# Sums of rows packed into four column groups, and the mean of h moved one column tile earlier, in a graph-attention plus mixture-of-experts kernel

## The chip, the cores and the metric

The kernel runs on one core of one Trainium2 chip. The metric is the device time of one execution in microseconds (us); the median of three runs before the change is 1255.57 us. Engines are named as in the profile: PE is TensorE (PEld its weight loads), DVE is VectorE, ACT is ScalarE, POOL is GpSimd, SP is SyncE.

## What is computed

Cut to what matters here (N = 4096 nodes, 256 features, 4 heads of 64):

```
xn   = layernorm(x)
h    = einsum('nd,hdk->hnk', xn, W)
e    = leaky_relu(s_row[:, :, None] + s_col[:, None, :]);  e = where(adj > 0, e, -9e15)
att  = softmax(e);   out = att @ h  (heads side by side)
y    = elu(out) + xn @ Wr + br;   x = x + layernorm(y)
x    = x + moe_ffn(layernorm(x))         # 8 experts, the best 2 for each token
```

A row of `adj` without any edge gives equal attention to all nodes, so its result is the mean of h. The kernel provides for that with a tiny constant: it adds `hbar = TINY * sum-of-xn/N @ W` to every numerator and `TINY` to every denominator. The mean of h needs the sum over all 4096 rows of xn. That small side computation is all that the change touches.

## The kernel before

**Stages.** An opening prepares the first two blocks of 512 nodes by hand. Then come four row blocks of attention (`for a in range(NR)`, each for 1024 target rows in two halves of 512), each running over 32 column tiles `j` of 128 source nodes. After that the experts' layers run, one tile of 256 rows after another.

**One column tile** (lines 1195 to 1238 and 1697 to 1706): DVE makes four weight tiles `w` (L1701, one per head, 128x1024 for both halves; 128x512 where only one half is done), in ten rotating buffers. PE multiplies them: `acc` (L1202, two 32-column pieces of h per head and half) and `den` (L1211, two columns of `unit` per head and half). The pieces are placed in the four 32-column groups of the array so that four run side by side. In the first and the last tile of a row block `attend` takes `other_heads` before `first_heads`, so that `acc` of heads 2 and 3 and `den` are done first. ACT turns the adjacency into a mask `am` for each tile (L1618, three buffers).

**The opening** (`first_phase`, L924 to 1024): block 0 and block 1 are centred, turned and projected without being scaled by 1/deviation first; the factor r is put in later. So their sums of rows can't come for free from the copies that turn the blocks; `sums_of_centred` (L874) takes them with products. For each of 8 pieces (two blocks of 4 x 128 rows) it multiplies the piece by its column of r, one row of 256 results in PSUM, all 8 accumulated in it. DVE copies that row out (L884). After the first half tile the row is turned by two transposes into `pc` (L891), which DVE copies into `sums[:, :, 0]` (L892). Both functions put their PE instructions into the strict PE order (`order_of`, `queue`).

**The other blocks** 2 to 7: `norm_steps` (L1035) measures a block, `normal_row` (L777) scales its four pieces on ACT with `off` and `r` from DVE (`off` is L769), and PE turns them (`pt`, L784); the copies out of PSUM (L800) sum the rows into `sums[:, :, b]`. `project_steps` (L1092) makes `ph` (L1105) and `pr` (L1057). These steps are placed between column tiles of row block 0 by `prepare_at`. The last block's step is over at column tile j = 27 of row block 0.

**The mean of h** (`mean_of_h`, L1171): DVE adds up `sums` into `xm` (L1174, L1175), PE makes four products of 128x128 weights with one column (`pm`, L1179), DVE scales them into `hbar` (L1183). It is called once, after the last column tile of row block 0. Then `finish_blocks` starts: ACT moves `den` out (`ud`, L1410) and the four `acc` banks (`u`, L1413, adding `hbar`), and PE's next row block accumulates into the same banks, so it waits for those copies.

**Who sets the order.** PE's order is written by hand: every PE instruction of the attention goes through `queue`. In the opening every engine keeps the order of the program (`in_trace_order`). After it, DVE, ACT, POOL and SP get their order from the framework's scheduler when the kernel is built; each engine then runs its list in order and waits at an instruction whose inputs or buffers are not ready. PSUM tiles named by `bank` rotate through three banks.

Of the kernel before, what the change touches and what calls it, by code (L numbers as in the profile page):

```python
# [14 lines left out]
OP = mybir.AluOpType  # L15
# [3 lines left out]
P = 128  # L19
# [25 lines left out]
def gat_then_moe(  # L45
# [19 lines left out]
    nc = tc.nc  # L65
    N, D = x.shape
    H, _, K = W.shape
    E, _, F = W1.shape
    NT = N // P
# [19 lines left out]
    TB = B // P  # L89
    HK = H * K  # L90
    Q = 32
# [11 lines left out]
    ident = const.tile([P, P], F32)  # L103
# [4 lines left out]
    parts = nc.dram_tensor("parts", [NB, H, B], F32, kind="Internal").ap()  # L108
# [110 lines left out]
    def forward(apart, stack):  # L219
# [13 lines left out]
        def large(name):  # L233
            return home[0].tile([P, TB, D], F32, tag="large", name=name, bufs=3)
# [10 lines left out]
        def bank(shape, name):  # L245
            return ps.tile(shape, F32, tag="bank", name=name, bufs=3)
# [286 lines left out]
        def queue(ins):  # L533

            if last[0] is not None:
                tc.add_manual_dep(
                    ins.ins, last[0],
                    mybir.DependencyInfo(
                        mybir.DependencyClass.NoSync, mybir.DependencyReason.DATA
                    ),  # L540
                    reason="the order of the tiles in TensorE",
                )
            last[0] = ins.ins.name
# [3 lines left out]
        def order_of(ins):  # L547

            if ordered[0] or strict[0]:
                queue(ins)  # L550
            return ins.ins
# [67 lines left out]
        with ExitStack() as layer:  # L619
# [42 lines left out]
            all1f = gat.tile([P, P], F32)  # L662
# [46 lines left out]
            def bounds_checked():  # L709

                nc.vector.tensor_reduce(strayed, limit, AX.X, OP.max)
                nc.vector.tensor_scalar(strayed, strayed, 0.5 * SPREAD, None, op0=OP.is_gt)
# [16 lines left out]
            sums = gat.tile([P, DC, NB], F32)  # L729
# [143 lines left out]

            def sums_of_centred(blocks):  # L874

                po = bank([1, D], "po")
                parts = [(xb, r, t) for xb, r in blocks for t in range(TB)]
                for n, (xb, r, t) in enumerate(parts):
                    order_of(nc.tensor.matmul(
                        po, r[:, t : t + 1], xb[:, t, :],  # L880
                        start=(n == 0), stop=(n + 1 == len(parts)),
                    ))
                row = large("row")[:1, 0, :]
                nc.vector.tensor_copy(row, po)  # L884
                return row

            def sums_turned(row):

                pc = bank([P, DC], "pc")
                for c in range(DC):  # L890
                    order_of(nc.tensor.transpose(pc[:, c : c + 1], row[:, ts(c, P)], ident[:1, :1]))  # L891
                nc.vector.tensor_copy(sums[:, :, 0], pc)  # L892
                nc.vector.memset(sums[:, :, 1], 0.0)

            def product_of(b, t, ph):
# [183 lines left out]
            def numbers_made():  # L1079

                if not apart:
                    nc.vector.tensor_scalar(brm, brm, -1.0, None, op0=OP.add)
                made_of_numbers()
# [87 lines left out]
            def mean_of_h():  # L1171

                xm = small.tile([P, DC], F32, tag="xm", name="xm", bufs=1)
                nc.vector.tensor_reduce(xm, sums, AX.X, OP.add)  # L1174
                nc.vector.tensor_scalar(xm, xm, 1.0 / N, None, op0=OP.mult)  # L1175
                pm = bank([P, H // 2], "pm")
                for i in range(H // 2):
                    for c in range(DC):
                        order_of(nc.tensor.matmul(  # L1179
                            pm[:, i : i + 1], wall[:, c, ts(i, P)], xm[:, c : c + 1],  # L1180
                            start=(c == 0), stop=(c == DC - 1),
                        ))
                nc.vector.tensor_scalar(hbar, pm, TINY, None, op0=OP.mult)  # L1183
# [438 lines left out]
            if not apart:  # L1622

                with tc.tile_pool(name="gen", bufs=2) as work:
# [12 lines left out]
                    for b in range(NB):  # L1637
# [4 lines left out]
                        for j in range(NT):  # L1642
# [6 lines left out]
                            for h in range(H):  # L1649
                                nc.vector.scalar_tensor_tensor(  # L1650
                                    top[:, h, :], off, eb[:, j, h : h + 1], top[:, h, :],
                                    op0=OP.add, op1=OP.max,
# [5 lines left out]
                            mx, mx, SLOPE, mx, op0=OP.mult, op1=OP.max  # L1658
                        )
                        for j in range(NT):  # L1660
# [7 lines left out]
                            for h in range(H):  # L1668
                                nc.vector.tensor_scalar(
                                    w[:, h, :], rows[:, h, :], eb[:, j, h : h + 1], None,  # L1670
                                    op0=OP.add,
                                )
                            nc.vector.scalar_tensor_tensor(
                                w, w, SLOPE, w, op0=OP.mult, op1=OP.max
# [16 lines left out]
            else:  # L1691

                with tc.tile_pool(name="sep", bufs=2) as work:

                    def weigh(er, am, j, halves):
                        these = slice(halves[0], halves[-1] + 1)
                        mask = am.rearrange("p (s r) -> p s r", s=HB)
                        w = [[None] * H for half in range(HB)]
                        for h in ORDER:
                            wh = work.tile([P, HB, B], F32, tag="w", name="w", bufs=10)  # L1700
                            marks["w"] = nc.vector.scalar_tensor_tensor(  # L1701
                                wh[:, these], er[:, these, h], eb[:, j, h : h + 1], mask[:, these],
                                op0=OP.max, op1=OP.min,
                            ).ins
                            for half in range(HB):
                                w[half][h] = wh[:, half]
                        return w

                    both = list(range(HB))
                    ers = [er0, er1]  # L1710
                    er = er0
                    pending = None
                    norms, steps_of = {}, {}
                    ordered[0] = strict[0] = True
                    opened = len(nc.cur_bb.bb.instructions)
                    row = first_phase(weigh, norms)
                    in_trace_order(opened)
                    ordered[0] = False
                    with tc.issue_after(marks["w"]):
                        numbers_made()  # L1720
                        bounds_checked()

                    def prepare_at(s):

                        for b in range(2, NB):
                            first = TB * b
                            if first - 3 <= s < first:
                                if b not in norms:
                                    norms[b] = norm_steps(b)
                                next(norms[b], None)  # L1730
                            if first <= s < first + 4:
                                if s == first:
                                    steps_of[b] = project_steps(b, True)
                                next(steps_of[b], None)

                    for j in range(TB):
                        prepare_at(TB + j)
                        attend(weigh(er, first_masks[:, j], j, [1]), j, [1])
                        if j == 0:
                            sums_turned(row)  # L1740
                    for a in range(NR):
                        later = None
                        for j in range(0 if a else TB, NT):
                            attend(
                                weigh(er, load_mask(a, j), j, both), j, both,
                                False if (a, j) == (NR - 1, NT - 1) else None,
                            )
                            if a == 0:
                                prepare_at(TB + j)
                            if pending:  # L1750
                                next(pending, None)
                            if a == 1 and j == 1:
                                turn_biases()
                            if a + 1 == NR and j == 3:
                                with tc.issue_after(marks["w"]):
                                    plan_early()
                                first_tile()
                            if a + 1 == NR and j == 25:
                                turn_first()
                            if a + 1 == NR and j == NT - 1:  # L1760
                                gelu_next(xT0[:, DC - 1, :1])
                            if j == 20 and a + 1 < NR:
                                later = ers[(a + 1) % 2]
                                load_rows(later, (a + 1) * HB, HB, nc.scalar)
                        if a == 0:
                            mean_of_h()
                        er = later
                        if a + 1 < NR:
                            pending = finish_blocks(a)
                            next(pending)  # L1770
                    strict[0] = False
# [359 lines left out]
```

## Time and profile before

| | |
|---|---|
| median of three runs | 1255.57 us (1255.51 to 1255.64) |
| the profiled execution | 1254.18 us, of which the profile's span is 1252.5 us |
| PE busy in the span | 1237.9 us (99%) |
| DVE busy | 845.1 us (67%) |
| ACT busy | 448.2 us (36%) |
| POOL busy | 241.8 us (19%) |
| chain that ended last | PE 94%, DVE 3% of the span |
| sums of rows in the opening (L879) | 16 PE instructions, 43.0 to 46.7 us |
| mean of h (L1179) | 8 PE instructions, first at 255.1, last at 255.9 us |
| row block 0 to 1 | about 255 to 258 us |

How to read it: times are microseconds from the start of the span. A product in fp32 shows as two PE records (the eight products at L879 are 16 records). A line of the timeline gives start, length, engine, source line, operation, output<-inputs, shapes and count, and in brackets the idle time of the engine before it with what ended it. The end of a PE record is modelled, so the distance between the starts of successive records tells the pace better than their length. In the chain and wait views, "issue" is time for which the profile shows no cause.

### The profile page before, as it was taken

What the parts mean: (1) busy time and instruction counts of PE and PEld (TensorE: products, weight loads), DVE (VectorE), ACT (ScalarE), POOL (GpSimd) and SP (SyncE); (2) the same over time, 40 slices, a digit from 0 to 9 for tenths busy, and PEclk for the clock granted to TensorE, in tenths of its full rate; (3) what the DMA queues carried; (4) which work ended last, traced back from release to release, by engine and by line L of the source; (5) the groups of instructions that cost most, each with busy time, mean ns of one, the idle gap of its engine ahead of it and who ended that gap; (6) DMA issues with size and microseconds to landing.
All of it is one profiled execution on the core that took longest, in us unless ns stands there. A gap on an engine that the chain in (4) does not pass through costs nothing.

```text
span 1252.5 us, 22714 instructions
## 1 busy us (share of the span) xinstructions
PE 1237.9 (99%) x8872; PEld 647.5 (52%) x8872; DVE 845.1 (67%) x1566; ACT 448.2 (36%) x918; POOL 241.8 (19%) x217
## 2 busy tenths in 40 slices
PE   9999999999999999999999999999999999999997
PEld 5444444332233332332324423888888876666686
DVE  7998887879999989999999996855111211111110
ACT  4332322165522375322645321533323332222322
POOL 4000000001002601006110015124432222222222
PEclk9999999999999999999999999999999999999999
DMA  6333433436533746334366422868999895455662
GB/s 216 118 119 111 164 114 102 150 121 133 187 105 102 236 114 206 103 102 153 113 159 200 128 81 91 273 169 217 229 251 252 222 230 119 106 137 112 135 163 32
DMA packets 155540, 190.22 MB, mean 152 GB/s; under 512 B 72312, under 2 KB 125680, under 8 KB 155040
## 3 DMA queue, kind: packets, MB, share of 16 engines
q1 hardware_dynamic: 133392, 145.39, 40.1%
q0 software_dynamic: 20544, 36.74, 13.3%
q10 hardware_dynamic: 1488, 6.55, 1.5%
q8 instruction: 71, 1.16, 0.4%
q14 instruction: 45, 0.37, 0.1%
HBM read 155.77 MB, written 29.74 MB: 148 GB/s over the span
## 4 chain that ended last, share of the span: by engine, by line
PE 94%; DVE 3%; issue 1%; ACT 1%; DMA 0%; POOLq 0%; SPq 0%; DVEq 0%; ACTq 0%
PE acc L1202 33%; PE po L1919 18%; PE ph L1885 17%; PE den L1211 17%; PE pr L1057 2%; DVE w L1701 2%; PE ph L1105 2%; PE ptx L1257 0%; DMA early<-lists 0%; PE acc L898 0%; PE pt L784 0%; PE ptr L1503 0%; PE po L1958 0%; PE pl L1268 0%; PE acc L748 0%
## 5 line engine op out<-in xcount | busy, mean ns | idle before, releaser
L1202 PE MATMUL acc<-w,ha 128*32 128x512 f32 x4096 | 669.9, 593 | 1.3 <-ACT u L1413 0.9
L1701 DVE SCALAR_TENSOR_TENSOR w<-er,eb,am 128x1024 f32<-128x1024 f32 x496 | 606.0, 1275 | 31.1 <-PE den L1211 30.9
L1211 PE MATMUL den<-w,unit 128*2 128x512 f32 x2048 | 467.0, 592 | 0.1
L1202 PEld LDWEIGHTS acc<-w,ha 128*32 128x32 f32 x4096 | 184.9, 110 | 292.4 <-issue 253.7
L1618 ACT ACTIVATE am<-adj 128x1024 bf16<-128x1024 int32 x124 | 130.7, 1054 | 346.2 <-DVE w L1701 211.7
L1885 PE MATMUL ph<-xT,w 128*128 128x256 f32 (+5 forms) x864 | 229.9, 423 | 0.2 <-ACT hT L1889 0.2
L1919 PE MATMUL po<-w,hT 128*128 128x256 f32 (+1 forms) x1040 | 229.7, 379 | 0.0
L1889 ACT ACTIVATE hT<-ph,bias 128x256 f32<-128x256 f32 (+5 forms) x216 | 111.1, 517 | 288.1 <-issue 186.2
L1919 PEld LDWEIGHTS po<-w,hT 128*128 128x128 f32 (+1 forms) x1040 | 195.7, 189 | 31.2 <-issue 3.1
L1885 PEld LDWEIGHTS ph<-xT,w 128*128 128x128 f32 x864 | 163.5, 190 | 59.7 <-issue 38.0
L1932 DVE SCALAR_TENSOR_TENSOR o<-po,share,b2s 128x256 f32<-128x256 f32 (+2 forms) x66 | 31.5, 478 | 210.9 <-PE po L1919 182.8
L1211 PEld LDWEIGHTS den<-w,unit 128*2 128x2 f32 x2048 | 93.7, 85 | 148.1 <-issue 139.7
L1944 POOL DMA_INDIRECT out<-o,ids x66 | 102.6, 1554 | 323.3 <-DMA out<-o,ids 141.5
L1388 POOL DMA_INDIRECT lists<-xe,at x64 | 89.3, 1395 | 267.6 <-issue 184.2
L1869 DVE STREAM_TRANSPOSE xT<-xr 128x512 f32<-128x512 f32 (+5 forms) x21 | 17.9, 851 | 70.9 <-PE ph L1885 31.2
L1057 PE MATMUL pr<-wr,xT 128*128 128x256 f32 x128 | 30.4, 381 | 0.2 <-ACT er L1151 0.2
L1907 ACT ACTIVATE b2s<-b2b,share 128x256 f32<-128x256 f32 x68 | 30.0, 499 | 0.0
L1125 POOL DMA_DIRECT2D residual<-rb x6 | 4.7, 784 | 121.2 <-DVE rb L1072 121.2
L1453 POOL DMA_DIRECT2D xf<-in_x x6 | 8.1, 1345 | 102.2 <-ACT xf L1452 102.2
L1057 PEld LDWEIGHTS pr<-wr,xT 128*128 128x128 f32 x128 | 24.1, 190 | 5.4 <-issue 0.9
L1105 PE MATMUL ph<-wall,xT 128*128 128x264 f32 x96 | 24.6, 399 | 0.0
L207 ACT ACTIVATE m<-y,off 128x256 f32<-128x256 f32 x48 | 23.7, 494 | 1.1 <-DVE off L215 0.6
(394 smaller groups left out, 616.4 us busy)
## 6 DMA issues: line engine op xcount, KB each, us to landing
adj<-in_adj SPq DMA_DIRECT2D x126, 512.0 KB
w<-in_L_ffn_W SPq DMA_DIRECT2D x54, 1024.0 KB
er<-parts ACTq DMA_DIRECT2D x3, 2048.0 KB
lists<-zeros POOLq DMA_DIRECT2D x8, 520.0 KB
residual<-rb POOLq DMA_DIRECT2D x8, 512.0 KB
rb<-residual SPq DMA_DIRECT2D x8, 512.0 KB
out<-y POOLq DMA_DIRECT2D x8, 512.0 KB
xb<-in_x SPq DMA_DIRECT2D x7, 512.0 KB
```

The costliest lines, as they stand in the source:

```text
L1057: order_of(nc.tensor.matmul(pr[:, k, :], turned[b][:, c, ts(t0 + k, P)], wr[:, c, :], start=(c == 0), stop=(c == DC - 1),))
L1105: order_of(nc.tensor.matmul(phs[t - t0], xT[:, c, ts(t, P)], wall[:, c, :], start=(c == 0), stop=(c == DC - 1),))
L1202: queue(nc.tensor.matmul(acc[half][h // 2][here : here + Q, :], ha[:, j, h * K + g * Q : h * K + (g + 1) * Q], w[half][h], start=(j == 0), ...
L1211: queue(nc.tensor.matmul(den[here : here + HB, :], unit[:, j, h, 1 - half : 1 - half + HB], w[half][h], start=(j == 0 and half == 0), stop ...
L1388: ins = nc.gpsimd.indirect_dma_start(lists, bass.IndirectOffsetOnAxis(ap=at[:, k, t : t + 1], axis=0), xe[:, t, :], None,).ins
L1618: nc.scalar.activation(am, at, AF.Relu, scale=2.0)
L1701: marks["w"] = nc.vector.scalar_tensor_tensor(wh[:, these], er[:, these, h], eb[:, j, h : h + 1], mask[:, these], op0=OP.max, op1=OP.min,).ins
L1885: order_of(nc.tensor.matmul(ph, job["w1"][:, c, ts(f, P)], xT[:, c, :], start=(c == 0), stop=(c == DC - 1),))
L1889: job["gelu"] = nc.scalar.activation(hT[:, f, :], ph, AF.Gelu, bias=job["bias"][:, f : f + 1]).ins
L1919: order_of(nc.tensor.matmul(po[:size], hT[:, f, k * CH : k * CH + size], w2[:, f, :], start=(f == 0), stop=(f == FC - 1),))
L1932: given_out.append(nc.vector.scalar_tensor_tensor(o[:size], po[:size], share[:size, k : k + 1], b2s[k][:size], op0=OP.mult, op1=OP.add,).ins)
L1944: added.append(add().ins)
```

## The change

The sums of the first two blocks are taken by the same eight products, but each with its column of r repeated 32 times, and the four pieces of a block go to four different groups of 32 PSUM partitions. So PSUM holds 128 rows: 32 equal copies of four partial sums. The DVE copy takes 128 rows. Turning the row is now a product with a column of ones over all 128 partitions, which adds the four partial sums 32 times over; the DVE instruction that stores the result scales it by 1/32. Separately, `mean_of_h` is called after column tile 30 of row block 0 in place of after tile 31.

```diff
-                po = bank([1, D], "po")
-                parts = [(xb, r, t) for xb, r in blocks for t in range(TB)]
-                for n, (xb, r, t) in enumerate(parts):
-                    order_of(nc.tensor.matmul(
-                        po, r[:, t : t + 1], xb[:, t, :],
-                        start=(n == 0), stop=(n + 1 == len(parts)),
-                    ))
-                row = large("row")[:1, 0, :]
+                po = bank([P, D], "po")
+                for n, (xb, r) in enumerate(blocks):
+                    for t in range(TB):
+                        order_of(nc.tensor.matmul(
+                            po[ts(t, Q)], r[:, t : t + 1].to_broadcast([P, Q]), xb[:, t, :],
+                            start=(n == 0), stop=(n + 1 == len(blocks)),
+                        ))
+                row = large("row")[:, 0, :]
                 nc.vector.tensor_copy(row, po)
...
-                    order_of(nc.tensor.transpose(pc[:, c : c + 1], row[:, ts(c, P)], ident[:1, :1]))
-                nc.vector.tensor_copy(sums[:, :, 0], pc)
+                    order_of(nc.tensor.matmul(
+                        pc[:, c : c + 1], row[:, ts(c, P)], all1f[:, :1], start=True, stop=True
+                    ))
+                nc.vector.tensor_scalar(sums[:, :, 0], pc, 1.0 / Q, None, op0=OP.mult)
...
                             if a == 0:
                                 prepare_at(TB + j)
+                            if (a, j) == (0, NT - 2):
+                                mean_of_h()
...
-                        if a == 0:
-                            mean_of_h()
```

## The prediction

> **What bounds the kernel now.** I read the page first: its busy times and the chain that ended last.
>
> ```profile
> PE 1237.9 (99%) x8872; PEld 647.5 (52%) x8872; DVE 845.1 (67%) x1566; ACT 448.2 (36%) x918; POOL 241.8 (19%) x217
> PE 94%; DVE 3%; issue 1%; ACT 1%; DMA 0%; POOLq 0%; SPq 0%; DVEq 0%; ACTq 0%
> ```
>
> PE is the chain nearly everywhere, and its order is fixed by hand. So what PE is spared anywhere before 773 us moves all that follows, as long as nothing else becomes late. Next, the timeline of the opening's end:
>
> ```profile
> 43.03 2.97 PE L879 MATMUL po<-xb,rrow 128*1 128x256 f32 x13
> 43.93 2.73 DVE L1701 SCALAR_TENSOR_TENSOR w<-er,eb,er 128x512 f32<-128x512 f32 x4
> 45.84 0.59 PE L879 MATMUL po<-xb,rrow 128*1 128x256 f32 x2
> 46.27 0.38 PE L879 MATMUL po<-xb,rrow 128*1 128x256 f32 x1
> 46.69 0.41 DVE L884 COPY row<-po 1x256 f32<-1x256 f32 x1
> 47.03 2.72 DVE L1701 SCALAR_TENSOR_TENSOR w<-er,eb,er 128x512 f32<-128x512 f32 x4
> 49.15 0.28 PE L891 MATMUL pc<-ident,row 1*128 1x1 f32 x2
> 49.36 1.06 PE L1202 MATMUL acc<-w,ha 128*32 128x512 f32 x8
> ```
>
> The reader is to see 16 records of `po` one after the other, 0.216 us apart (43.03 to 46.27 in 15 steps), all in the first column group, and DVE without a pause beside them. The waits of DVE from 43 to 99 us hold only one of 0.3 us, before 43.14; PE has none put down to another engine in 43 to 256 us. From 100 us DVE waits for PE again and again (17 times, 14.8 us, at `w`, behind `den`): from there PE alone sets the pace. Last, the border of row blocks 0 and 1, and ACT at the next border, 1 to 2:
>
> ```profile
> 255.12 1.05 PE L1179 MATMUL pm<-xm,wall 128*128 128x1 f32 x8
> 256.10 1.03 PE L1211 MATMUL den<-w,unit 128*2 128x512 f32 x4
> 257.12 0.15 DVE L1183 TENSOR_SCALAR hbar<-pm 128x2 f32<-128x2 f32 x1
> 257.31 2.42 ACT L1413 ACTIVATE u<-acc,hbar 128x512 f32<-128x512 f32 x4 [0.16 <-DVE hbar L1183]
> 258.05 0.62 PE L1202 MATMUL acc<-w,ha 128*32 128x512 f32 x2 [0.92 <-ACT u L1413]
> ```
>
> ```profile
> 428.70 0.69 ACT L1413 ACTIVATE u<-acc,hbar 128x512 f32<-128x512 f32 x1 [0.36 <-PE acc L1202]
> 429.56 0.69 ACT L1413 ACTIVATE u<-acc,hbar 128x512 f32<-128x512 f32 x1 [0.17 <-PE den L1211]
> 430.14 0.68 ACT L1410 ACTIVATE ud<-den,tiny 128x512 f32<-128x512 f32 x1
> ```
>
> At the first border `hbar` sits on DVE behind three `w` and ends at 257.27; the copies `u`, and PE's first `acc`, follow it. At the second, where `hbar` is long there, the copies run while PE is still at the last tile.
>
> [...] the router's 32-column products `pl` (L1268) of 128 columns issue 32 records from 366.34 until `acc` follows at 367.22, 0.11 us for each four. [...] Here the trace shows two `pc` transposes as 2 records, and four `pm` products as 8: an fp32 product costs twice the records.
>
> **The opening, part by part.**
>
> *Products.* 16 records x 0.216 = 3.46 us become 4 rounds of four records. If they run side by side as `pl` and `acc` do (acc rounds are 0.429 us apart at 512 columns), that is 4 x 0.216 = 0.86 us: 2.6 us less. Weight loads of 32 columns take 110 ns against 84, but lie beside products, as in `acc`. If the groups did not overlap the gain would be 0; I take 2.6.
>
> *What is late next: w.* In the built order of the changed kernel the row copy stands before the last of the four `w` of the next half tile (the first three were made by 42 us); before, it stood four `w` later. The copy now waits for `po`: last record 43.68, end 44.06, copy at 44.12 in place of DVE being free at 43.93, a pause of 0.19. It takes a slot of 0.34 (46.69 to 47.03; one partition or 128 should be alike: `ha`, 128x256, takes 0.42 against 0.41 here). So that `w` runs from 44.46 to 45.20. PE, free of `po` at 43.90, does `den` and `acc` of heads 1, 0, 2 until 44.76, then waits for head 3 until 45.25: 0.5 us of the gain lost (the cost today is nothing, because the longer `po` covers it).
>
> *Turning.* Two transposes cost 0.21 (49.15 to 49.36); four records of full products at the pace of `pm` (0.98 for eight) cost 0.49: 0.28 more. `sums` is read far later, at 208 us; a scaling of 128x2 takes 0.152 (hbar) against 0.143 for the copy.
>
> Sum: -2.6 + 0.5 + 0.28 = -1.8 us on PE at about 49 us.
>
> *Does it last until DVE has slack?* PE runs 1.8 earlier, DVE about 0.1 later. The tightest `w` I find in the DVE timeline against the tiles' starts is head 0 of tile 4: ready 55.52, used 58.27, a slack of 2.75. It holds. The second risk is a reordering. In the changed build the statistic `off` of block 3 (81.40 now) stands behind one more `w`, and ACT does the next mask before the four rows of `xb`, not after:
>
> ```profile
> 81.59 2.08 ACT L777 ACTIVATE xb<-xb,off,r 128x256 f32<-128x256 f32 x4 [4.40 <-DVE off L769]
> 83.58 1.04 ACT L1618 ACTIVATE am<-adj 128x1024 bf16<-128x1024 int32 x1
> ```
>
> Today the rows are ready at 83.67 and PE turns them from 86.78: slack 3.1. Changed: that `w` runs to 82.6 (81.48 + 1.27 + about 0.25 of pauses at `sc` and `ha`, less 0.41 for two small instructions that stand later now), the mask 82.65 to 83.7, the rows 83.6 to 85.8; PE wants the last of them at 85.7 (86.78 - 1.8 + 6 x 0.109). So 0.2 us of waiting, within 0 to 0.7 if the DVE pauses are 0.7. After 95 us slack is large again: block 4's rows end by 101 us and are turned at 116 us. I take -1.6 for the opening, ends -1.0 and -1.8. The two earlier `x` loads on SP follow `po` by dependence and are not needed before 62 us.
>
> **The border, part by part.** The eight `pm` records, with the array running empty before them, cost PE 1.1 us (255.01, when the next round was due, to 256.10). Between tiles 30 and 31 they cost the same, since that border is an unbroken stream too: 0. `xm` is done at 208 us, so nothing waits there. What goes is PE's wait: `den` begins at 256.10, `acc` at 258.05, and from 258.05 the tile takes its full 12 rounds (its end at 263.21 is 5.16 later, 12 x 0.429 = 5.15), so the early `den` bought nothing: 1.95 us are lost today. In the changed order `hbar` stands behind the first `w` of tile 1 of the next row block; that is the one at 250.75 today, so `hbar` is made at about 252.1, and `u` can start when heads 2 and 3 are summed, about 253.7. The order of `u`, `u`, `ud`, `u`, mask, `u` is then that of the border 1 to 2, where PE loses nothing: first `den` at 431.06, one round after the last `acc` at 430.63. Gain 1.95; were a copy late by a mask's 1.06 us it would be 0.9, and more than 1.95 can't be had because nothing else waits.
>
> **Sum.** -1.6 - 1.95 = -3.55 us. Against the profiled execution (span 1252.5, total 1254.18): 1250.6; it lies 1.39 us under the median of the runs, so 1255.57 - 3.5 = 1252.1 is what I predict. About 0.2% (2.5 us, down to 1253.06) is what a measurement of this kernel can tell from no change.
>
> **Rivals.**
> 1. *DVE eats the opening's gain.* For: DVE has no pause from 43 to 99 us. Against: its lead is 2.75 us or more. If the pauses add up and PE waits at block 3's turn for 1.2 us more, the opening gives 0.4: 1253.2.
> 2. *The border stays closed for another reason*, say a mask ahead of `u` on ACT. For: a mask of 1.06 stood in front of it (256.09). Against: the border 1 to 2. Only the opening counts: 1254.0.
> 3. *The full opening gain, no wait at block 3 or for head 3*: -2.3 - 1.95: 1251.3.
> 4. *Slower.* The one mechanism: block 3's rows on ACT, behind `off`, one more `w` and a mask, are so late that PE, whose order is strict, stands before `pt`. It costs 1 us for each us beyond 85.7, and outweighs both gains (3.75) when the last row ends after 89.5, that is, when `off` slips by 5 us and not 1.2; two more `w` and a round trip to ACT would do it. At 5 us of waiting: 1256.8.
> 5. *The change doesn't do what it says*: groups not side by side, and the turning dearer: opening +0.3, border -1.95: 1253.9.
>
> **Chances.** Forecast 0.62 (own range 1251.6 to 1252.7); rival 1 0.16, of which half is beyond 1253.06; rival 2 0.08; rival 3 0.06; rival 4 0.05; rival 5 0.03. Faster by over 0.2%: 0.62 + 0.06 + 0.08 = 0.76; within: 0.08 + 0.08 + 0.03 = 0.19; slower 0.05. The range takes in forecast, rivals 3 and 1: 1251.2 to 1253.7.
>
> **What would show it.** `po` records in fours, 0.216 apart, over by 44.1; a PE pause before head 3's `acc` near 44.8; `pc` near 47.1 with four records; the turn of block 3 near 85, with or without a pause; `hbar` near 249 to 252, `u` before the last `acc` of row block 0, and no pause of PE at that border. I am wrong if PE stands before `pt` for over 1 us, if `po` runs in a row, or if the copies `u` still begin after the last tile.

## The result and the profile after

The changed kernel takes 1251.76 us (median of six runs, 1250.76 to 1252.48) against 1255.61 us of the kernel before (median of six): a ratio of 0.9973, 95% interval 0.9962 to 0.9983. Run again in a later set it took 1251.07 us (1250.89 to 1251.43) against 1255.29, ratio 0.997 (0.9958 to 0.9982). The profiled execution of the changed kernel took 1252.34 us with a span of 1250.3. In what follows line numbers of the changed kernel are those of before plus 2 from `sums_turned` on: `acc` is L1204, `w` L1703, `pm` L1181, `hbar` L1185, `u` L1415. Three stages will come up again and again: the *opening* (up to the end of the turning of the sums, about 50 us), the *turn of block 3* (PE turning that block's rows, `pt`, about 87 us) and the *border* between row blocks 0 and 1 (about 255 us). The first product behind the border that belongs to the finished row block is `pd`. Products in the four 32-column groups (`acc`, `den`, now `po`) are called packed, the others (`pt`, `pc`, `pm`, and `pp`, which turns a block's factors) full-array.

The page of the changed kernel, its busy times and the shares of the chain that ended last:

```profile
PE 1235.8 (99%) x8874; PEld 647.2 (52%) x8874; DVE 845.5 (68%) x1566; ACT 448.6 (36%) x918; POOL 242.1 (19%) x217
PE 94%; DVE 3%; issue 1%; DMA 1%; ACT 1%; POOLq 0%; SPq 0%; DVEq 0%; ACTq 0%
```

Hardly anything here tells of the change: PE has two more records (the turning has four in place of two) and is busy 2.1 us less. The page sums over the whole run, so the gain has to be read stage by stage. I take the same PE step in both traces and subtract: how much earlier or later does it start?

| PE's step, at its time before | after minus before, us | what lies behind it |
|---|---|---|
| 8.5 (`pt`, block 0) | -0.26 | start of this execution |
| 20.1 to 43.0 (`po` begins) | +1.36 | halved clock from 8.5 to 12.0, see below |
| 52.1 to 86.8 | -0.31 | opening: -1.67 |
| 93.0 to 234 | -0.24 | turn of block 3: +0.07 |
| 263.3 (`pd`) to 784 | -2.17 | border of row blocks 0 and 1: -1.93 |

A minus sign means earlier. The three stages that the change touches sum to -3.53 us. The step of +1.62 to the second row isn't the change's: PE reaches the first changed product only at 43 us, and the view by windows shows TensorE's clock there. Its columns are the window, its length, then the busy time and count of PE, PEld, DVE, ACT and POOL, the granted clock, the DMA share and GB/s. The first line is the kernel before, the others are the changed kernel:

```profile
9.00:10.00 1.00, 1.00 (x7) 0.87 (x7) 0.83 (x7) 0.58 (x1) 1.00 (x2) 1.00 1.10 376
9.00:10.00 1.00, 1.00 (x3) 0.78 (x3) 0.83 (x6) 0.59 (x1) 1.00 (x3) 0.50 1.10 374
10.00:11.00 1.00, 1.00 (x5) 0.79 (x4) 0.02 (x1) 0.00 (x0) 1.00 (x2) 0.50 1.02 389
11.00:12.00 1.00, 1.00 (x4) 0.90 (x5) 0.58 (x7) 0.00 (x0) 0.62 (x2) 0.52 1.01 414
```

The clock reads 0.50: PE is "busy" all the time and gets about half as much done, 12 records in these three windows against 22 in the kernel before, where the clock is 1.00 throughout. I call such a stretch of halved clock a *spell*. So these two executions differ by 1.6 us for a reason that lies ahead of the changed code, and their times (1254.18 and 1252.34) must not be subtracted as they stand.

The opening's end in the timeline of the changed kernel:

```profile
44.40 1.07 PE L879 MATMUL po<-xb,rrow 128*32 128x256 f32 x16
45.53 0.43 DVE L884 COPY row<-po 128x256 f32<-128x256 f32 x1 [0.15 <-PE po L879]
45.88 3.39 DVE L1703 SCALAR_TENSOR_TENSOR w<-er,eb,er 128x512 f32<-128x512 f32 x5
46.67 0.62 PE L1204 MATMUL acc<-w,ha 128*32 128x512 f32 x2 [0.35 <-DVE w L1703]
48.51 0.61 PE L891 MATMUL pc<-all1f,row 128*128 128x1 f32 x4
49.05 1.06 PE L1204 MATMUL acc<-w,ha 128*32 128x512 f32 x8
```

All 16 `po` records start within 1.07 us, where they had been 0.216 apart; the next `acc` starts at 45.28, so they cost 0.88. Then DVE stands 0.15 us for `po`, copies the row, and only then makes the next `w`; PE, which had started a round at 45.71, starts the next at 46.67 and not 0.43 later: 0.53 us lost, and the trace names `w` as the releaser. The turning costs 0.54 (48.51 to 49.05).

The turn of block 3:

```profile
84.07 1.06 ACT L1620 ACTIVATE am<-adj 128x1024 bf16<-128x1024 int32 x1 [4.02 <-DVE off L769]
85.03 2.06 ACT L777 ACTIVATE xb<-xb,off,r 128x256 f32<-128x256 f32 x4
86.47 1.11 PE L784 MATMUL pt<-ident,xb 128*128 128x128 f32 x8
```

ACT does the mask first and the rows of the block after it, as the built order had said. The last rows are scaled while PE is already turning the first: the slack of 3.1 us is used up, and PE waits 0.07 us.

The border of row blocks 0 and 1:

```profile
249.74 1.05 PE L1181 MATMUL pm<-xm,wall 128*128 128x1 f32 x8
251.71 0.15 DVE L1185 TENSOR_SCALAR hbar<-pm 128x2 f32<-128x2 f32 x1
253.52 0.69 ACT L1415 ACTIVATE u<-acc,hbar 128x512 f32<-128x512 f32 x1 [1.78 <-PE acc L1204]
255.87 0.60 PE L1213 MATMUL den<-w,unit 128*2 128x512 f32 x2
255.91 0.60 PE L1204 MATMUL acc<-w,ha 128*32 128x512 f32 x2
```

`hbar` is done 1.7 us before `u` starts (251.86 against 253.52), and `u` now waits for `acc`, as at the later borders. The first `acc` of the next row block follows in the same round as its `den`; before, it came 1.95 us behind it.

### The profile page after: what moved, and what is told of

Read it like the earlier page. It is cut to its first block, busy times and chain, and to the rows that moved or that the text cites. A ratio compares the mean times of both kernels' runs of the same rounds, so it can differ in the third digit from the quotient of the medians.

```text
span 1250.3 us, 22717 instructions
## 1 busy us (share of the span) xinstructions
PE 1235.8 (99%) x8874; PEld 647.2 (52%) x8874; DVE 845.5 (68%) x1566; ACT 448.6 (36%) x918; POOL 242.1 (19%) x217
## 4 chain that ended last, share of the span: by engine, by line
PE 94%; DVE 3%; issue 1%; DMA 1%; ACT 1%; POOLq 0%; SPq 0%; DVEq 0%; ACTq 0%
PE acc L1204 34%; PE po L1921 18%; PE ph L1887 17%; PE den L1213 17%; PE pr L1059 2%; DVE w L1703 2%; PE ph L1107 2%; PE acc L900 1%; PE ptx L1259 0%; DMA early<-lists 0%; PE pt L784 0%; PE ptr L1505 0%; PE po L1960 0%; PE pl L1270 0%; DMA xb<-in_x 0%
## 5 line engine op out<-in xcount | busy, mean ns | idle before, releaser
L1204 PE MATMUL acc<-w,ha 128*32 128x512 f32 x4096 | 669.7, 593 | 0.8 <-DVE w L1703 0.8
L1703 DVE SCALAR_TENSOR_TENSOR w<-er,eb,am 128x1024 f32<-128x1024 f32 x496 | 606.5, 1277 | 27.2 <-PE den L1213 27.2
L1204 PEld LDWEIGHTS acc<-w,ha 128*32 128x32 f32 x4096 | 184.3, 110 | 291.4 <-issue 253.3
```

The costliest lines, as they stand in the source:

```text
L1204: queue(nc.tensor.matmul(acc[half][h // 2][here : here + Q, :], ha[:, j, h * K + g * Q : h * K + (g + 1) * Q], w[half][h], start=(j == 0), ...
L1703: marks["w"] = nc.vector.scalar_tensor_tensor(wh[:, these], er[:, these, h], eb[:, j, h : h + 1], mask[:, these], op0=OP.max, op1=OP.min,).ins
```

## The experiments

Each ratio below is to runs of the kernel before on the same chip. Since spells come and go (the changed kernel's first six runs lie around 1250.97 and 1252.41 us, 1.44 apart), the table at the end compares only runs with a mean granted clock of at least 0.998; one spell of 3.4 us at half pulls the mean of 1250 us down by 0.0014. Where a step is said to move "at 94.9 us", that is its time in the kernel before. The absolute times that I expected for the first set were reckoned from 1255.57 us, but there the kernel before ran at 1254.36; so products only, mean only and one group all came out 0.9 to 1.6 us faster than expected, one group even under the 1252.9 that its rival named. These times decide nothing; the stages do.

**One half each.** The products alone (`mean_of_h` put back behind the loop):

```diff
-                            if (a, j) == (0, NT - 2):
-                                mean_of_h()
...
+                        if a == 0:
+                            mean_of_h()
```

> Only the four-group products and their turning; the mean of h stays after tile 31. My theory (opening 1.6 us, border 1.95 us, added): PE is 1.6 us earlier from the turn of block 3 (about 87 us) on, against the kernel before and apart from any stretch of halved PE clock at the start; at the border of row blocks 0 and 1 PE again waits 1.9 us for the copies u. Time 0.3 us to 0.5 either side of 1254.0. Rival (the opening's gain is taken up by DVE, the border brings all): no shift at 87 us, time as before. Rival (what was gained is only the clock at the start): shift 0.

Measured: 1253.14 us, ratio 0.9991 (0.9983 to 1.0). PE is at +0.18 before `po`, at -1.50 from 52 to 86.8 us, at -1.42 from 93 us on, and at -1.42 still at `pd` (263 us). The border in its timeline:

```profile
253.70 1.05 PE L1181 MATMUL pm<-xm,wall 128*128 128x1 f32 x8
255.70 0.15 DVE L1185 TENSOR_SCALAR hbar<-pm 128x2 f32<-128x2 f32 x1
255.89 2.42 ACT L1415 ACTIVATE u<-acc,hbar 128x512 f32<-128x512 f32 x4 [0.16 <-DVE hbar L1185]
```

`u` waits for `hbar`, as before; the opening's gain goes through this border whole and closes nothing there.

The mean alone (the same move, made in the kernel before):

> Only the mean of h after tile 30; products of one row as before. My theory: nothing moves up to 249 us, pm costs PE 1.1 us between tiles 30 and 31, the copies u begin at about 253.5 us, PE doesn't pause at the border, and all that follows is 1.95 us earlier: time about 1253.6. Rival (the border stays closed for another reason, such as a mask ahead of u on ACT): 0 to 0.9 us earlier.

Measured: 1251.98 us, ratio 0.9982 (0.9976 to 0.9989). PE stands at -0.08 up to 234 us and at -2.00 at `pd`. The border is worth 1.93 us by itself, as it is in the changed kernel, so the two parts add.

**Not side by side.** All eight products into the first group of 32 columns, so that they cost what they did, with the dearer turning kept:

```diff
-                po = bank([P, D], "po")
+                po = bank([Q, D], "po")
...
-                            po[ts(t, Q)], r[:, t : t + 1].to_broadcast([P, Q]), xb[:, t, :],
+                            po, r[:, t : t + 1].to_broadcast([P, Q]), xb[:, t, :],
...
-                row = large("row")[:, 0, :]
+                row = large("row")[:Q, 0, :]
```

> As the changed kernel, but all eight products of 32 equal columns go into the one 32-partition group, one after the other; turning over 32 partitions. My theory: the 16 records of po are again 0.216 us apart (3.46 us), so the opening gives nothing and loses about 0.3 us by the dearer turning; with the border about 1.6 us are left: time about 1253.9. Rival (the gain comes from fewer or smaller DVE copies or from the new order on DVE, not from groups side by side): the opening keeps 1 us or more, time under 1252.9.

Measured: 1252.66 us, ratio 0.9987 (0.998 to 0.9993). Its timeline:

```profile
43.10 2.99 PE L879 MATMUL po<-xb,rrow 128*32 128x256 f32 x13
46.36 0.38 PE L879 MATMUL po<-xb,rrow 128*32 128x256 f32 x1
49.24 0.60 PE L892 MATMUL pc<-all1f,row 32*128 32x1 f32 x4
```

With 32 equal columns in place of one the products take as long as before, first to last record 3.26 us against 3.24: here the columns cost nothing, and the gain of the products lies in the four groups alone. The opening is at +0.34, which is the dearer turning (predicted +0.28); PE doesn't pause before head 3. The border is at -1.93 again.

**The pause before head 3.** The row is copied only behind the last `w` of the half tile, and turned one half tile later:

```diff
+                with tc.issue_after(marks["w"]):
                     nc.vector.tensor_copy(row, po)
...
                         if j == 0:
+                            row = sums_kept(row)
+                        if j == 1:
                             sums_turned(row)
```

> As the changed kernel, but the copy of the row out of PSUM stands behind the fourth w on DVE and the turning comes one half tile later. My theory: the pause of PE before head 3 (0.5 us) is due to that copy alone and goes; the opening then gives 2.1 us, all 0.5 us under the changed kernel, unless block 3's rows on ACT are late by the same 0.5. Rival (the pause is the cost of starting the 32-column products after the sums): the pause stays, time as the changed kernel.

Measured: 1251.27 us, ratio 0.9973 (0.9963 to 0.9984): no better than the changed kernel, and for a reason. Up to 65 us PE is at -2.41, so the opening now gives 2.45 and not 1.67, more than the 2.1 that I expected. But at 94.9 us it is at -1.27. Its timeline, the turning first and then the turn of block 3:

```profile
49.22 0.60 PE L896 MATMUL pc<-all1f,row 128*128 128x1 f32 x4
49.69 1.07 PE L784 MATMUL pt<-ident,xb 128*128 128x128 f32 x8
82.68 1.06 ACT L1625 ACTIVATE am<-adj 128x1024 bf16<-128x1024 int32 x1 [4.02 <-DVE r L181]
83.98 2.08 ACT L777 ACTIVATE xb<-xb,off,r 128x256 f32<-128x256 f32 x4 [0.24 <-DVE off L769]
84.64 1.92 PE L784 MATMUL pt<-ident,xb 128*128 128x128 f32 x8
```

Of the 0.78 us that the opening gains on the changed kernel, 0.53 are the pause, which is gone. Another 0.20 come from the new place of the turning: it stands right ahead of the full-array transposes of block 2. From the round due before them to the next packed round, turning and transposes cost 1.58 us here, and 0.65 and 1.14 apart in the changed kernel.

At block 3 the eight transposes take 1.92 us in place of 1.04 to 1.11: PE takes each row as ACT delivers it. PE came 0.78 us earlier than in the changed kernel, and the rows came later: on DVE `off` now stands behind one more `w` and ends at 83.94, where the second execution of the changed kernel has 82.75, so ACT waits for it after the mask and starts the rows at 83.98 and not at 83.73. In all 1.14 us are given back. This is the mechanism of the prediction's rival 4, at a size of 1.14 and not the 3.75 that it needed.

**Away with that wait.** The late copy, and besides it block 3's statistics and scaling one column tile sooner, its turning where it was:

```diff
-                        if first - 3 <= s < first:
+                        if first - 3 - (b == 3) <= s < first:
...
                     normal_row(found, t)
                 yield
+                if b == 3:
+                    yield
                 pt = banks_turned()
```

> The changed kernel with two edits: the row of sums is copied out of its bank only after the last w of the opening's tile (as in the kernel with the late copy, where that brought 2.45 us up to 86.7 us and lost 1.14 of it at the turn of block 3), and the statistics and the normalization of block 3 are issued one column tile sooner, its turning where it was. Theory: the 1.14 us were the wait of TensorE, held to a strict order, for block 3's rows on ScalarE, which came late behind VectorE's off; with off and the rows some 5 us sooner that wait is gone. So pt of block 3 at -2.4 and the products behind it at -2.3 to -2.5, pd of the first finished block at -4.2 to -4.4, span 2.0 to 0.9 us below that of the changed kernel, time 1250.1 to 1250.9 where the late copy alone has 1251.27 and the changed kernel 1251.76. Rival: the wait isn't for the rows but for something else at that place (the factors' part for pp, the bank of pt), or the statistics a tile sooner make VectorE wait for the block's load or give it more to do where it is short; then 1.0 to 1.2 us are lost again by 95 us (-1.3 there), and the time is that of the late copy.

Measured: 1250.66 us (1249.82 to 1252.83), ratio 0.997 (0.9958 to 0.9982); three of its six runs had a spell; the three without had 1249.82 to 1250.08, where the changed kernel has 1250.76 to 1251.43. PE is at -2.41 from 65 to 222 us without a break, and at -4.34 at `pd`. At the turn:

```profile
82.77 1.06 ACT L1627 ACTIVATE am<-adj 128x1024 bf16<-128x1024 int32 x1 [3.73 <-DVE w L1710]
84.38 1.04 PE L784 MATMUL pt<-ident,xb 128*128 128x128 f32 x8
```

The rows are scaled long before, from 74.54 us on, and the transposes take 1.04 us. So the wait in the late-copy kernel was for the rows, and what DVE does earlier for them made nothing else late.

**What the early mean still costs.** In the changed kernel the next packed round was due at 249.62, 0.43 us after the last, and begins at 250.72: `pm` costs 1.10 us inside the packed stream. Here it is put right behind the last turning of factors `pp` (after tile 27), where PE changes from packed to full-array products anyway:

```diff
-                            if (a, j) == (0, NT - 2):
+                            if (a, j) == (0, NT - 1 - TB):
```

> The changed kernel, but the mean of h is taken after column tile 27 instead of 30, right behind the turning of block 7's last factors, where TensorE has gone from packed products to a full-array one anyway. My theory: what the early mean still costs inside the row block is the passage of TensorE from the packed products to the mean's eight full-array products and back, and beside the turn that passage is already paid. So the opening stays as in the changed kernel (pt, pp of block 3 at -0.3 against before), and pd of the first finished block (263 us before) stands 2.2 to 2.4 us earlier than before, 0.0 to 0.2 more than the 2.17 of the changed kernel; time 1251.5 to 1251.8 where the changed kernel has 1251.76. The rival: the mean is only a matter of having left the border, its place inside makes no difference (2.17, same time); or h isn't complete by then and a wait for the last scaled rows appears at pm (pm's first weight load waits, pd less than 2.0 earlier).

Measured: 1250.68 us, ratio 0.997 (0.9959 to 0.998). Against the same execution's own stand at the turn of block 3, `pd` comes 2.26 us earlier, not 1.93: 0.33 more. My expectation was too low there (0 to 0.2), and its absolute figures (2.2 to 2.4 for `pd`, and the time) were reckoned from an execution and a median with the spell in them; without it `pd` is at -4.25.

```profile
232.19 0.28 PE L1159 MATMUL pp<-ident,part 128*16 128x128 f32 x1
232.30 0.95 PE L1181 MATMUL pm<-xm,wall 128*128 128x1 f32 x8
233.18 1.92 PE L1204 MATMUL acc<-w,ha 128*32 128x512 f32 x16
```

The round due at 232.07 begins at 233.18: 1.11 for `pp` and `pm` together, hardly more than for `pm` alone. In the changed kernel `pp` costs 0.32 by itself (due 233.83, begun 234.15), so beside `pm` it is all but free. That is as it should be if what costs is PE's way from packed to full-array products and back, gone once here and not twice. The turning of the sums in the late-copy kernel, put beside block 2's transposes and 0.20 us cheaper there, fits this too.

**The halved clock.** The second warm-up at 7 us with three products in place of one, so that PE's pause before `pw` is filled:

```diff
-                warm_up(1)
+                warm_up(3)
```

> The changed kernel with three products of the second warm-up instead of one: it fills TensorE's pause at 6.7 to 7.3 us with work that nobody reads. In the profiled execution of the changed kernel the granted clock was halved from 8.4 to 11.8 us, in that of the kernel before it was not, and the times of every kernel so far fall into two groups 1.4 to 1.6 us apart. Theory: the halved spell is what parts the groups, and a pause of TensorE just ahead of it brings it on; then this kernel shows one group only, near 1251.0 to 1251.4 (the lower group of the changed kernel, 1250.76 to 1251.19, and at most 0.4 for the two added products), and a clock without a spell at half. Rival: the spell comes whatever TensorE does in that pause; then both groups stay, the higher at 1252.4 to 1252.9, and a profiled execution of the higher group has the spell.

Measured: 1250.91 us, six runs from 1250.72 to 1251.17, no spell. That would be the theory's answer, but the changed kernel, run in the same set, had none in six runs either:

> The changed kernel once more, on the chip on which the others of this set run, so that they can be compared with it and not only with the kernel before. Expected: 0.9972 of the kernel before, opening -1.6, border -1.9, and the two groups of times, 1250.8 to 1251.2 and 1252.3 to 1252.5, the granted clock at the start telling which group the profiled execution belongs to.

Measured: 1251.07 us; the two groups that I expected were one. Its profiled execution: opening -1.68, turn of block 3 +0.08, border -1.93, which is the first trace once more without the +1.62. For the clock the two runs decide nothing, so I took the warm-up product away:

> The changed kernel without the one product of the second warm-up, so that TensorE's pause at 6.3 to 7.5 us grows by the 0.35 to 0.39 us that this product takes. Theory (pause brings the spell on): most runs are in the higher group, 1252.2 to 1252.6, and a profiled execution there has the granted clock at half for 3.4 us at about 8 to 12 us. Rival: the spell's coming doesn't hang on this pause (the kernel with the mean beside the turn had a pause of about 0.6 us there and no spell); then the groups are mixed as in the changed kernel, the lower at 1250.8 to 1251.4.

Measured: 1252.48 us, ratio 0.9985 (0.9977 to 0.9993). Nine of 13 runs are below a mean clock of 0.998, and the times lie in three steps: 0.998 and more at 1251.09 (median), 0.996 to 0.997 at 1252.48, 0.995 at 1254.12. The profiled execution is of the last kind, with the clock at half for 6.83 us, two spells in a row, from 7.7 us, behind a pause of 0.92 us. So with a longer pause the spell came more often: on this chip the kernel with all three edits, whose pause is the usual one, had it in 1 run of 5. And the other way round, in the kernel before:

> The kernel before with three products of the second warm-up instead of one. The kernel before has had about as many runs at 1253.7 to 1254.4 as at 1254.8 to 1256. Theory: with the pause filled only the lower group is left, 1253.7 to 1254.6, and the median stands about 1 us below that of the kernel before. Rival: both groups stay, in about equal numbers, the higher at 1255.2 to 1255.9, and the median is that of the kernel before within 0.5 us.

Measured: 1254.29 us, ratio 1.0001 (0.9993 to 1.001), seven runs without and six with a spell: the theory's forecast of one group failed. The profiled execution, one of the six, shows where one spell stood; the windows view, and the first `acc` of row block 1:

```profile
256.00:258.00 2.00, 1.08 (x9) 0.15 (x12) 2.00 (x3) 1.84 (x3) 0.00 (x0) 1.00 0.00 0
258.00:260.00 2.00, 2.00 (x12) 0.45 (x16) 0.33 (x1) 1.59 (x3) 0.00 (x0) 0.56 0.81 223
```

```profile
257.91 0.78 PE L1202 MATMUL acc<-w,ha 128*32 128x512 f32 x2 [0.92 <-ACT u L1413]
```

The start is clean, but 0.34 us after PE's pause at the border (0.92, for `u`) the clock drops to half, from 258.25 to 261.66, and PE loses 1.70 us against the kernel before at 263 us. So a spell also came right behind the border's pause, the one that the change removes. That it was the pause that brought it on is a guess from this one execution; in the profiled execution of the kernel before the same pause was followed by none.

**All together.** Late copy, rows sooner and the mean at the turn:

> The two edits of the last set put together: the row of sums copied after the last w of its tile with block 3's statistics and rows a column tile sooner (opening -2.41 us alone), and the mean of h right behind the last turning of factors (border -2.26 alone). Theory: they touch different stages and add up: -2.4 at 94.9 us, -4.6 to -4.7 at pd of the first finished block, lower group of times at 1249.4 to 1249.8, some 0.3 us below the kernel with the late copy and sooner rows and 1.3 below the changed kernel. Rival: the opening's gain and the border's gain share a cause (work that VectorE or ScalarE has stored up by the border), and together they bring no more than the better of them, -4.3.

Measured: 1249.6 us (1249.35 to 1251.08), ratio 0.9961 (0.9948 to 0.9975). Its profiled execution has a spell at the start; apart from that the opening gives 2.45, nothing is lost at block 3, and the border gives 2.26: they add up. With three warm-up products too:

> The kernel with all three, and three warm-up products instead of one at 7 us. The kernel with the three products alone showed one group of times in six runs, but so did the changed kernel in the same set, so that says little yet. Theory: filling TensorE's pause keeps the granted clock from being halved at the start; then all runs lie in one group at 1249.4 to 1249.9 and none 1.3 to 1.6 above it. Rival: the spell comes as often as without, and some of the runs are at 1250.9 to 1251.4.

Measured: 1249.48 us (1249.05 to 1249.66), ratio 0.996 (0.9946 to 0.9974), no spell in five runs. It is the fastest version of the study, about 1.6 us below the changed kernel; without a spell it is no faster than the one before it (1249.55).

The stages are from each kernel's profiled execution; the last column is the median of the runs whose mean clock is at least 0.998, and how many of all runs they are.

| kernel | opening | turn of block 3 | border | without a spell, us (runs) |
|---|---|---|---|---|
| before (in three sets) | | | | 1254.03, 1254.05, 1253.97 (60 of 92) |
| changed (both sets) | -1.67, -1.68 | +0.07, +0.08 | -1.93, -1.93 | 1251.04 (9 of 12) |
| products only | -1.68 | +0.08 | 0.00 | 1252.97 (10 of 13) |
| mean only | 0.00 | 0.00 | -1.93 | 1251.93 (16 of 21) |
| one group | +0.34 | 0.00 | -1.93 | 1252.31 (14 of 21) |
| late copy | -2.45 | +1.14 | -1.93 | 1251.22 (7 of 8) |
| late copy, rows sooner | -2.45 | 0.00 | -1.93 | 1249.85 (3 of 6) |
| mean at the turn | -1.68 | +0.08 | -2.26 | 1250.53 (6 of 8) |
| three warm-up products | -1.68 | +0.08 | -1.93 | 1250.91 (6 of 6) |
| no second warm-up | -1.68 | +0.08 | -1.93 | 1251.09 (4 of 13) |
| all three | -2.45 | 0.00 | -2.26 | 1249.55 (4 of 5) |
| all three, warm-up | -2.45 | 0.00 | -2.26 | 1249.48 (5 of 5) |
| before, three warm-up products | 0.00 | 0.00 | 0.00 (+1.70 by the clock) | 1253.89 (7 of 13) |

## Why the prediction was right

By its own steps, predicted against measured:

- *Products*: predicted -2.6; the records need 0.88 us (predicted 0.86). Right, and the kernel with one group, with 3.26 us from its first record to its last, shows that the four groups are the whole of it.
- *Head 3's `w`*: +0.5; measured 0.53, with DVE's pause 0.15 (predicted 0.19). The late copy shows that it is the cost of the copy's place: with the copy moved the pause is gone.
- *Turning*: +0.28; measured 0.54 against 0.21, so +0.33, and +0.34 in the kernel with one group, where nothing else in the opening costs more or less. A little low: I priced the four records at the pace of `pm` (0.12 each). That pace spreads the 0.18 us from the last full-array record to the next packed round over eight records; here four bear it.
- *Block 3's turn*: +0.2 within 0 to 0.7; measured +0.07. The mechanism is the one described, with the mask ahead of the rows. The late copy shows how near it was: with 0.78 us more of a lead for PE and rows 0.25 us later, 1.14 are lost.
- *The border*: -1.95; measured -1.93. My term for the early `pm`, "they cost the same: 0", holds for its new place between tiles 30 and 31 (1.10 before and after), but it isn't a fixed price: beside `pp` the two together are 0.3 us cheaper. The prediction didn't see that.
- *The sum*: -3.55 predicted, -3.53 from the stages.

The rivals: DVE has not eaten the gain (rival 1: +0.07 at block 3), the border opened (2), and the groups ran side by side (5: 0.88 us for the 16 records). Rival 3's full opening gain wasn't there, but was to be had by the late copy and sooner rows.

What was less sound is the last step, from the profiled execution to the median. I added 1.39 us because the runs of before lay that much above its profiled execution. All three runs shown lay in the range (1255.2 to 1256) where 28 of the 32 runs with a spell lie in the later sets, and only 3 of the 60 without; the profiled execution had no spell. Of the changed kernel's first six runs half had one. So the median of 1251.76 lies between two groups, 1250.97 and 1252.41, and 1252.1 came close to it partly by that chance.

Like with like, without a spell, the gain is 1254.02 - 1251.04 = 3.0 us, 0.5 less than the stages say. Most of this difference is a term that the prediction didn't have: the part of a run's time that lies outside the profile's span. There the runs of the kernel before have 1.6 to 1.8 us (92 runs) and those of the changed kernel 2.0 to 2.2 (12 runs), so about 0.4 us of the gain are lost there, and that belongs to the kernel and isn't chance; the spans alone differ by 3.4 us (medians 1252.3 and 1248.9, without a spell). The loss comes with the products and not with the mean: products only has 2.0 to 2.2, mean only 1.6 to 1.8, and so have one group (1.6 to 1.8) and, but for single runs up to 2.0, the kernels with the late copy (1.7 to 1.8). What causes it no run shows. From 777 to 794 us, where the experts' layers begin, PE moved by -0.15 us in one execution of the changed kernel and by +0.26 in the other; that is chance.

## What to carry to other kernels

When a hand-ordered engine is given time back, look at once for what arrives there late next: here 0.5 us hung on where one copy stood on DVE, and moving it only brought out the next wait, of 1.1 us for rows on ACT, until those were made sooner too. Put small full-array products beside others, so that PE leaves its packed products once for both: that was worth 0.3 us for `pm` and 0.2 for the turning. And before two executions are subtracted, compare their granted clock: 1.6 us, nearly half of this gain, came from a spell that was over before the changed code began.

## What was not expected of the hardware

The granted clock fell to half in four of the 14 profiled executions: for 3.41 us in the changed kernel (8.54 to 11.95 us, at a cost of 1.62 us), in the kernel with all three and in the kernel before with three warm-up products (258.25 to 261.66 us, 1.70 us), and for 6.83 us in the kernel with no second warm-up. The end of the span, where the clock reads half too (from 1249.45 us in the kernel before, from 1244.16 in the changed one), is left aside. By their mean clock (below 0.998), runs of nearly every kernel had such spells. In the 3.41 us ahead of the spells PE was busy for 2.73, 2.71, 1.97 and 2.49 us (changed kernel, all three, no second warm-up, before with three warm-up products), with single pauses of 0.6 to 0.9 us. But 2.49 us of work from 256.15 to 259.56 us, at the border of the kernel before, was followed by no spell, nor was 2.45 from 4.19 to 7.60 us in the kernel with the mean at the turn. So the busy time alone doesn't decide it.

Nor does the length of the pause. Where the warm-up was left as it was, PE paused before `pw` for 0.59 us in the profiled executions of the changed kernel and of all three, and a spell followed; it paused for 0.59 with the mean at the turn and for 0.55 in the changed kernel's second execution, and none followed. The pause isn't the kernel's own either: it is 0.15 us in the kernel before, where the four `ptw` ahead of it take 1.06 us and the warm-up product starts at 7.00, and 0.59 in the changed one, where they take 0.60 and it starts at 6.33; from 6 to 8 us the kernel with the late copy has PE idle for only 0.26. So kernels can't be sorted by their pauses alone, and what brings a spell on isn't settled.

Counted over all runs by what each kernel was meant to have: with both pauses (before) 32 of 92 runs whose clock is on record had a mean below 0.998, and 3 of 13 of the products alone; with the border's pause alone 6 of 13; with the start's alone 22 of 81 (changed kernel in both sets, mean only, one group, and the four kernels made from it that left the warm-up as it was); with a longer one at the start 9 of 13; with neither none of 11. In the sets of these 11 the kernels that differ from the changed one elsewhere, or not at all, had 6 of 25; if nothing had been changed, none in 11 would still come by luck about one time in eleven. So it isn't shown that filling the pause prevents the spell.
